# A mixture-of-experts and attention kernel: the first phase without filled expert queues, with on-chip counts, sixteen row buffers and splits placed behind other work

## The chip, the cores and the metric

The kernel runs on one core of one Trainium2 chip. A core has five engines with a queue each: TensorE (PE; its weight loads are listed as PEld), VectorE (DVE), ScalarE (ACT), GpSimd (POOL) and SyncE (SP, which here only issues DMA transfers). The metric is the device time in microseconds (us), the median of several executions. Before the change it is 1846.73 us (three runs, 1844.07 to 1847.13).

## The reference

The input `x` has 4096 tokens of 256 floats. Three steps are added to it one after the other: half a feed-forward layer, attention in groups of 64 tokens, half the same feed-forward layer again.

```python
x = x + 0.5 * ffn(layernorm(x))
x = x + attention(layernorm(x))     # groups of 64 tokens, 16 heads, causal
x = x + 0.5 * ffn(layernorm(x))

def ffn(x):                         # T = 4096 tokens, H = 256, E = 8 experts, 2 per token
    logits = rmsnorm(x) @ router_w.T
    p2, i2 = top_k(softmax(logits), 2);  rw = p2 / p2.sum()
    # each expert takes its first 640 tokens in order, the rest is dropped
    for e in experts:
        xg = x[dispatch[e]]                              # 640 x 256
        out = (silu(xg @ rg[e]) * (xg @ ru[e])) @ rd[e]  # 1024 hidden
        routed[dispatch[e]] += out * weight[e]
    shared = (silu(x @ sg) * (x @ su)) @ sd              # 2048 hidden, all tokens
    return shared + routed
```

## The kernel before

Each float32 operand of a matmul is split into a high and a low float16 plane, and three products (high-high, high-low, low-high, `TERMS`) stand for one. The split of a weight is one operation on ACT (high plane) and one on DVE (low plane): `split`, L102 and L103.

There are four phases, each a `with n.phase(...)` block. Phase a normalises all 32 tiles of 128 tokens, routes them, and runs the shared experts over the first four blocks of 512 tokens. Phase b runs the eight experts for the first layer. Phase c runs attention for 32 tiles, the routing of the second layer, and eleven blocks of shared experts. Phase d runs the experts of the second layer and the last shared block.

The **shared experts** of a block (`shared`) go in 16 chunks of 128 hidden units. A chunk is `gate_up` (twelve matmuls of 128x512 into two PSUM tiles `pgu`, L302; then silu on ACT, L313, into `sl`; product on DVE, L315; high plane `hh` on ACT, L317; low plane `hl` on DVE, L318) and `down` (twelve matmuls of 128x256 into `po`, L326). `down` of a chunk is deferred until `gate_up` of the next chunk has been issued.

The **front** of a tile (`tile1`, `front_steps`): load `y` (L629), statistics on DVE (L137 to L140), a power on POOL (L142), normalised `z` (L154), the two planes into a row buffer `X` (`two`: ACT L162, DVE L163), a transpose into `xb` (on PE for the first block, `turn`; by DMA for the others, L172), router matmuls and a copy of the logits on ACT (L207). After every fourth tile `route` picks the two best experts, counts positions with matmuls against a running count `run`, and computes the destination rows `di` (L268). `scatter` then writes four tag columns into `X` on POOL (L281: token number, two weights, first expert) and sends the 128 rows to the experts' queues `xg` in DRAM, twice, with an indirect DMA from POOL (L283). `X` has ten buffers in phase a, so the eleventh tile reuses the first one's once its scatters have landed.

The queues are **filled** beforehand (`fill`, L738 to L745): for each expert a zeroed tile with a token number beyond the end (so that an unused slot is dropped on the way back) is written to `xg`. The fill of the first layer stands in front of the blocks, that of the second layer beside block 2. The scatters of a layer come after its fills.

An **expert's load** (`expert_load`) reads a transposed copy of the queue (`xe`, L373) and the tag columns (`tag`, L375, two buffers), and makes the row indices `ids` on POOL (L380) and the weights `w` on DVE (L381, L383), each in two buffers. `experts` calls it for the next expert while one is computed; for the first expert it is called when all tiles are done.

Order of work: `Tiles.steps` advances the tiles that are alive; `drive` runs the yields of a shared block and lets the tiles take steps between them. The program text only gives a priority: a scheduler with a timeline of its own places each instruction on its engine's queue[...]. `issue_after` keeps an instruction behind another one in this placing. `load_shared` (L116) issues all loads and splits of the shared weights (8 steps of two chunks each, raw tiles in two buffers) before block 0 in the program's text.

Of the kernel before, what the change touches and what calls it, by code (L numbers as in the profile page):

```python
# [1 line left out]

# [18 lines left out]
P = 128  # L21
# [16 lines left out]
class Net:  # L38
    def __init__(self, ctx, tc):
        self.tc = tc  # L40
        self.nc = nc = tc.nc
        pool = lambda name, bufs, **k: ctx.enter_context(tc.tile_pool(name=name, bufs=bufs, **k))
        self.cst = pool("cst", 1)
        self.wsh = pool("wsh", 1)
        self.tok = pool("tok", YB)
        self.xb = pool("xb", NB)
        self.xe = pool("xe", 2)
        self.sm = pool("sm", 2)
        self.dr = pool("dr", 1, space=DRAM)
# [12 lines left out]
        for e in range(E):  # L62
            nc.gpsimd.memset(self.iota8[:, e:e + 1], float(e))
        self.mhalf = c.tile([P, 8], F32, name="mhalf")
        nc.gpsimd.memset(self.mhalf, -0.5)
        self.mone = c.tile([P, 4], F32, name="mone")
        nc.gpsimd.memset(self.mone, -1.0)
        self.e1 = c.tile([P, 4], F32, name="e1")
        nc.gpsimd.memset(self.e1, 2.718281828459045)
        tk = self.sm.tile([P, 32], I32, name="tk", bufs=1)  # L70
        nc.gpsimd.iota(tk, pattern=[[P, 32]], base=0, channel_multiplier=1)
        self.tokid = c.tile([P, 32], F32, name="tokid")
        nc.vector.tensor_copy(self.tokid, tk)
# [31 lines left out]

    def load_router(self, router_w):
        nc = self.nc
        r = self.raw.tile([E, H], F32, name="rtr", tag="raw2")
        nc.sync.dma_start(out=r, in_=router_w)
        self.rwt = self.cst.tile([P, 2, 2, E], F16, name="rwt")  # L110
        p = self.m1([P, 2, E], F32, "prt")
        for k in range(2):
            nc.tensor.transpose(p[:, k, :], r[:, k * P:(k + 1) * P], self.ident[:E, :E])
        self.split(self.rwt[:, 0], self.rwt[:, 1], p)

    def load_shared(self, sg, su, sd):  # L116

        nc = self.nc
        w = self.wsh
        self.sgu = w.tile([P, 16, 2, 2, 2, P], F16, name="sgu")  # L120
        self.sdw = w.tile([P, 2, 16, H], F16, name="sdw")
        for c in range(0, 16, 2):
            r = self.raw.tile([P, 2, 2, 2 * P], F32, name=f"rs{c}", tag="raw")
            for i, s in enumerate((sg, su)):
                nc.sync.dma_start(
                    out=r[:, i], in_=s[:, c * P:(c + 2) * P].rearrange("(k p) f -> p k f", p=P))
            for j in range(2):
                src = r[:, :, :, j * P:(j + 1) * P]
                self.split(self.sgu[:, c + j, 0], self.sgu[:, c + j, 1], src)
            r2 = self.raw.tile([P, 2, H], F32, name=f"rd{c}", tag="raw2")  # L130
            nc.sync.dma_start(out=r2, in_=sd[c * P:(c + 2) * P].rearrange("(k p) f -> p k f", p=P))
            self.split(self.sdw[:, 0, c:c + 2], self.sdw[:, 1, c:c + 2], r2)

    def stats(self, x, mv, rstd):
        nc = self.nc
# [5 lines left out]
            out=ve, in0=mv[:, 1:2], scalar1=LN_EPS, scalar2=1.0 / UP ** 2, op0=ALU.add, op1=ALU.mult)  # L141
        nc.gpsimd.tensor_tensor(out=rstd, in0=ve, in1=self.mhalf[:, :1], op=ALU.pow)  # L142

    def planes(self, x, xp, mv, rstd, pool=False):

        nc = self.nc
        z = self.tok.tile([P, H], F32, name="z", bufs=3)
        if pool:
            nm = self.sm.tile([P, 1], F32, name="nm")
            nc.vector.scalar_tensor_tensor(  # L150
# [2 lines left out]
        else:  # L153
            nc.vector.tensor_scalar(  # L154
                out=z, in0=x, scalar1=mv[:, 0:1], scalar2=rstd, op0=ALU.subtract, op1=ALU.mult)
        self.two(xp, z, pool)
        return z

    def two(self, xp, z, pool=False):
# [15 lines left out]
    def turn(self, z, xt):  # L175

        p = self.m1([P, 2, P], F32, "ptx")
        for k in range(2):
            self.nc.tensor.transpose(p[:, k, :], z[:, k * P:(k + 1) * P], self.ident)
        self.nc.scalar.copy(xt[:, 0:2], p)  # L180
        self.nc.vector.tensor_tensor(out=xt[:, 2:4], in0=p, in1=xt[:, 0:2], op=ALU.subtract)

    def front_new(self):
        fb = {"X": [None] * 4, "n": 0, "pe": False}
# [24 lines left out]
    def route(self, R, b, fb):  # L209
# [57 lines left out]
        di = sm.tile([P, 4, 2], I32, name="di")  # L267
        nc.vector.tensor_copy(di, df)  # L268
        yield
        for t in range(4):  # L270
            with self.tc.issue_after(self.anchor.ins) if self.anchor else nullcontext():
                self.scatter(R, b, fb, t, di, w1, dl, ef)
            yield

    def scatter(self, R, b, fb, t, di, w1, dl, ef):
        nc = self.nc
# [15 lines left out]
    def gate_up(self, wc, x, h, tanh=False):  # L292
# [4 lines left out]
        for i in range(2):  # L297
# [8 lines left out]
            if i == 0:  # L306
# [3 lines left out]
                    nc.vector.scalar_tensor_tensor(  # L310
                        out=s, in0=s, scalar=1.0, in1=p, op0=ALU.add, op1=ALU.mult)
                else:
                    nc.scalar.activation(s, p, AF.Silu, scale=1.0 / XP)  # L313
                yield
        nc.vector.scalar_tensor_tensor(  # L315
            out=s, in0=ps[1], scalar=1.0 / XP / (2.0 * XP if tanh else 1.0), in1=s, op0=ALU.mult, op1=ALU.mult)
        nc.scalar.copy(h[0], s)  # L317
        nc.vector.tensor_tensor(out=h[1], in0=s, in1=h[0], op=ALU.subtract)  # L318
        yield
# [49 lines left out]
    def expert_load(self, R, e, hold):  # L369
        nc = self.nc  # L370
        rows = R["xg"][e * CAP:(e + 1) * CAP]
        xt = hold["x"] = self.xe.tile([P, 4, CAP], F16, name="xe")
        nc.sync.dma_start_transpose(out=xt, in_=rows[:, 0:H].bitcast(F16))  # L373
        tag = self.sm.tile([P, 5, 4], F32, name="tag")
        nc.sync.dma_start(out=tag, in_=rows[:, H:XW].rearrange("(t p) f -> p t f", p=P))  # L375
        yield
        yield
        ids = hold["id"] = self.sm.tile([P, 5], I32, name="eid")
        w = hold["w"] = self.sm.tile([P, 5], F32, name="ew")
        nc.gpsimd.tensor_copy(ids, tag[:, :, 0])  # L380
        nc.vector.scalar_tensor_tensor(  # L381
            out=w, in0=tag[:, :, 3], scalar=float(e), in1=tag[:, :, 1], op0=ALU.is_equal, op1=ALU.mult)
        nc.vector.tensor_tensor(out=w, in0=w, in1=tag[:, :, 2], op=ALU.add)  # L383
# [85 lines left out]
    def attn_tile(self, R, j, x2, new_fb):  # L469
# [9 lines left out]
        self.stats(y, mv, rstd)  # L479
        yield  # L480
        xa = a.tile([P, 2 * H], F16, name="xa")
        self.planes(y, xa, mv, rstd, True)
        yield
        V2 = self.V2[j % 2]
        xt = self.flip(xa)
# [116 lines left out]
    def front_steps(self, y, t, new_fb, keep=None):  # L602
# [3 lines left out]
        X = self.xs.tile([P, XW], F32, name="X")  # L606
        xp = X[:, 0:H].bitcast(F16)
        fb["X"][t] = X
        z = self.planes(y, xp, fb["mv"][:, t, :], fb["rstd"][:, t:t + 1], keep is not None)
        xt = fb["xb"][:, :, t * P:(t + 1) * P]  # L610
        if fb["pe"]:
            self.turn(z, xt)
            fb["n"] += 1
            for _ in range((3 - t) * GAP_A + 1):
                yield
        if keep is not None:
            self.nc.sync.dma_start(out=keep, in_=y)
        yield
# [45 lines left out]
        self.slot += 1  # L664


def run_slots(tiles, until):
    while not until():
        for _ in tiles.steps():
# [23 lines left out]
def macaron(ctx, tc, x, w_qkv, ln_w, w_proj, router_w, rg, ru, rd, sg, su, sd, out):  # L693
# [7 lines left out]
    x2 = n.dr.tile([T, H], F32, name="x2")  # L701
    fbs = {}
    used = set()

    def new_fb(h, b):
        def get(t):
# [11 lines left out]
    def tile1(j):  # L718
        b, t = divmod(j, 4)
        y = n.load_tile(x, b, t)  # L720
        yield
        yield
        yield from n.front_steps(y, t, new_fb(1, b))
        yield from tail(R1, 1, b, t)

    def tile2(j):
        b, t = divmod(j, 4)
        yield from n.attn_tile(R1, j, x2 if b < NC else out, new_fb(2, b))
        yield from tail(R2, 2, b, t)

    def ready(h, b):
        return lambda: (h, b) in fbs and fbs[(h, b)]["n"] == 4
# [2 lines left out]
        yield from n.shared(b, fbs[key]["xb"], src, dst, **k)  # L735
        used.add(key)

    def fill(R):  # L738

        for e in range(E):  # L740
            z = n.raw.tile([P, 5, XW], F32, name="zero")
            nc.gpsimd.memset(z, 0.0)
            nc.vector.tensor_scalar_add(z[:, :, H], n.tokid[:, 0:5], float(T + e * CAP))
            nc.sync.dma_start(out=R["xg"][e * CAP:(e + 1) * CAP].rearrange("(t p) f -> p t f", p=P), in_=z)
            yield  # L745

    with n.phase("a", BT, 2, 10):
        n.ident = n.at.tile([P, P], F32, name="ident")
        make_identity(nc, n.ident)
        n.load_router(router_w)  # L750
        tiles = Tiles(tile1, 32, GAP_A)
        run_slots(tiles, ready(1, 0))
        n.load_shared(sg, su, sd)
        for _ in fill(R1):
            pass
        for b in range(NA):
            run_slots(tiles, ready(1, b))
            if b == 2:
                tiles.extra.append(fill(R2))
                for i in range(NA, NB):  # L760
                    nc.sync.dma_start(out=R1["acc"][i * BT:(i + 1) * BT], in_=x[i * BT:(i + 1) * BT])
            drive(all_shared((1, b), b, x, R1["acc"]), tiles, RATE_A)
        run_slots(tiles, tiles.done)
        cur = {}
        for _ in n.expert_load(R1, 0, cur):
            pass
    with n.phase("b", CAP, 3):
        n.experts(R1, rg, ru, rd, cur)
    with n.phase("c", BT, 2, 6, SLC):
        n.attn_init(w_qkv, ln_w, w_proj)  # L770
        tiles = Tiles(tile2, 32, GAP_C)
# [6 lines left out]
        cur = {}  # L778
        for _ in n.expert_load(R2, 0, cur):
            pass  # L780
    with n.phase("d", CAP, 3):
        n.experts(R2, rg, ru, rd, cur)
        for b in range(NC, NB):
            for _ in all_shared((2, b), b, out, out, late=10):
                pass
# [40 lines left out]
```

## Time and profile before

| What | Value |
|---|---|
| median of three runs | 1846.73 us |
| profiled execution | 1844.18 us, of which the span is 1842.5 us |
| phase a ends, phase b begins (PE) | 297.5 us |
| first matmul of shared experts | 14.10 us |
| granted PE clock | 0.999 of full speed |
| HBM | read 81.04 MB, written 52.85 MB |
| `xg<-zero` (fills) | 16 transfers of 650 KB |
| scatters L283 | 128, 1.03 us each on POOL |

The page gives per engine the busy time and its share of the span. A stage's row, as asked for by stretches of time, gives the same for a window. A wait is listed as "engine, line, waited for, us in total, times, longest". A row of the timeline is start, duration, engine, line, operation, output and inputs, count, and in brackets the idle time before it with what ended it.

### The profile page before, as it was taken

The numbers are of one execution on the slowest core, as the hardware profiler recorded it, in microseconds if no ns is written. First come the engines' busy times: TensorE is split into PE (matmuls) and PEld (weight loads), VectorE is DVE, ScalarE is ACT, GpSimd is POOL, SyncE is SP. The second block draws the span as 40 slices with busy tenths as digits, with TensorE's granted clock in tenths as the row PEclk, the third lists the DMA queues.
The fourth block names the chain that finished last, engine by engine and source line by source line (L and its number), as shares of the span: only waits on it lengthen the run. The fifth ranks groups of instructions, "written<-read, shape, count | busy, mean of one in ns | idle before, by whom it ended". The sixth has DMA issues, their size and how long they took to land.

```text
span 1842.5 us, 37619 instructions
## 1 busy us (share of the span) xinstructions
PE 1782.8 (97%) x13722; PEld 1197.0 (65%) x13722; DVE 1204.9 (65%) x2869; ACT 952.2 (52%) x2055; POOL 769.5 (42%) x1104
## 2 busy tenths in 40 slices
PE   6989999999999899999999999999999999999999
PEld 3545656777777556666666666666665677777765
DVE  7665545666666567787877878787755565666643
ACT  5333324555555365766666666666333455555542
POOL 7776540111221244567667676776530011112210
PEclk9999999999999999999999999999999999999999
DMA  9753022445554246767585776757213044455420
GB/s 291 224 142 94 12 63 69 107 107 114 128 115 101 58 80 110 118 114 158 104 148 117 140 137 119 152 98 125 48 30 87 27 111 111 108 112 127 104 47 12
DMA packets 447514, 196.61 MB, mean 107 GB/s; under 512 B 302369, under 2 KB 444381, under 8 KB 447264
## 3 DMA queue, kind: packets, MB, share of 16 engines
q1 hardware_dynamic: 429664, 173.03, 42.7%
q0 software_dynamic: 17664, 21.17, 6.7%
q8 instruction: 107, 1.75, 0.4%
q14 instruction: 79, 0.65, 0.1%
HBM read 81.04 MB, written 52.85 MB: 73 GB/s over the span
## 4 chain that ended last, share of the span: by engine, by line
PE 57%; POOL 12%; issue 11%; DVE 10%; DMA 5%; ACT 4%; SPq 1%; POOLq 0%; DVEq 0%; another core or an unknown queue 0%; ACTq 0%
PE pgu L302 36%; PE po L326 18%; POOL xg L283 3%; DVE sl L315 2%; DVE sl L310 1%; POOL X L281 1%; DVE hl L318 1%; POOL rstd L142 1%; POOL S L546 1%; DMA y<-in_L_attn_x_dram 1%; ACT hh L317 1%; PE pqk L599 1%; ACT sl L309 1%; POOL e L557 1%; DMA xg<-X,di 1%
## 5 line engine op out<-in xcount | busy, mean ns | idle before, releaser
L302 PE MATMUL pgu<-xb,sgu 128*128 128x512 f16 x3072 | 743.5, 380 | 20.3 <-DVE sl L310 8.0
L317 ACT CAST hh<-sl 128x512 f16<-128x512 f32 (+2 forms) x512 | 272.9, 533 | 485.4 <-DVE sl L315 471.4
L302 PE MATMUL pgu<-xe,wc 128*128 128x384 f16 (+1 forms) x3072 | 497.0, 299 | 0.8
L302 PEld LDWEIGHTS <-sgu 128*128 128x128 f16 x3072 | 294.0, 98 | 295.7 <-issue 29.6
L315 DVE SCALAR_TENSOR_TENSOR sl<-pgu,sl 128x512 f32<-128x512 f32 (+2 forms) x512 | 300.6, 587 | 215.5 <-PE pgu L302 180.1
L318 DVE TENSOR_TENSOR hl<-sl,hh 128x512 f16<-128x512 f32 (+2 forms) x512 | 311.0, 608 | 160.1 <-ACT hh L317 153.3
L326 PEld LDWEIGHTS <-hh 128*128 128x128 f16 x3328 | 319.8, 98 | 114.9 <-ACT hh L317 13.9
L302 PEld LDWEIGHTS <-wc 128*128 128x128 f16 x3072 | 300.5, 98 | 94.1 <-issue 1.9
L326 PE MATMUL po<-sdw,hh 128*128 128x256 f16 x2048 | 349.9, 273 | 10.1 <-ACT hh L317 6.8
L326 PE MATMUL po<-sdw,hl 128*128 128x256 f16 x1024 | 247.5, 273 | 11.7 <-DVE hl L318 10.4
L326 PE MATMUL po<-wd,hh 128*128 128x256 f16 x1280 | 223.6, 273 | 0.0
L326 PEld LDWEIGHTS <-hl 128*128 128x128 f16 x1664 | 162.8, 98 | 57.2 <-DVE hl L318 23.3
L422 POOL DMA_INDIRECT out_dram<-eo,eid x40 | 64.1, 1604 | 314.3 <-DVE hl L318 244.9
L313 ACT ACTIVATE sl<-pgu 128x384 f32<-128x384 f32 (+1 forms) x336 | 158.9, 473 | 56.7 <-PE pgu L302 27.6
L422 POOL DMA_INDIRECT acc<-eo,eid x40 | 64.8, 1621 | 266.2 <-DVE hl L318 227.4
L283 POOL DMA_INDIRECT xg<-X,di x128 | 131.3, 1026 | 66.2 <-issue 27.5
L326 PE MATMUL po<-wd,hl 128*128 128x256 f16 x640 | 152.5, 273 | 2.1 <-DVE hl L318 1.9
L310 DVE SCALAR_TENSOR_TENSOR sl<-sl,pgu 128x512 f32<-128x512 f32 x176 | 120.0, 682 | 45.4 <-ACT sl L309 43.2
L309 ACT ACTIVATE sl<-pgu 128x512 f32<-128x512 f32 x176 | 104.3, 593 | 42.3 <-PE pgu L302 36.3
L102 ACT ACTIVATE wc<-re 128x512 f16<-128x512 f32 x128 | 80.5, 629 | 78.0 <-PE pgu L302 51.2
L103 DVE SCALAR_TENSOR_TENSOR wc<-re,wc 128x512 f16<-128x512 f32 x128 | 88.3, 690 | 25.9 <-ACT wc L102 25.7
L546 POOL TENSOR_TENSOR S<-S,amx 128x1024 f32<-128x1024 f32 x32 | 62.1, 1939 | 79.1 <-DVE amx L545 72.1
(141 smaller groups left out, 1740.6 us busy)
## 6 DMA issues: line engine op xcount, KB each, us to landing
re<-in_L_ffn_rg_dram SPq DMA_DIRECT2D x128, 128.0 KB
re<-in_L_ffn_ru_dram SPq DMA_DIRECT2D x128, 128.0 KB
re<-in_L_ffn_rd_dram SPq DMA_DIRECT2D x128, 128.0 KB
xg<-zero SPq DMA_DIRECT2D x16, 650.0 KB
y<-acc SPq DMA_DIRECT2D x64, 128.0 KB
y<-in_L_attn_x_dram SPq DMA_DIRECT2D x32, 128.0 KB
acc<-xr SPq DMA_DIRECT2D x16, 256.0 KB
out_dram<-xr SPq DMA_DIRECT2D x16, 256.0 KB
```

The source lines that it names most:

```text
L103: nc.vector.scalar_tensor_tensor(out=lo, in0=src, scalar=WS, in1=hi, op0=ALU.mult, op1=ALU.subtract)
L283: i = nc.gpsimd.indirect_dma_start(out=R["xg"][:, :], out_offset=bass.IndirectOffsetOnAxis(ap=di[:, t, k:k + 1], axis=0), in_=X, in_offset ...
L302: nc.tensor.matmul(p, lhsT=wc[:, w, i, k, :], rhs=x[:, 2 * a + k, :], start=(j == 0), stop=(j == 5))
L309: nc.scalar.activation(s, p, AF.Tanh, scale=0.5 / XP)
L310: nc.vector.scalar_tensor_tensor(out=s, in0=s, scalar=1.0, in1=p, op0=ALU.add, op1=ALU.mult)
L313: nc.scalar.activation(s, p, AF.Silu, scale=1.0 / XP)
L315: nc.vector.scalar_tensor_tensor(out=s, in0=ps[1], scalar=1.0 / XP / (2.0 * XP if tanh else 1.0), in1=s, op0=ALU.mult, op1=ALU.mult)
L317: nc.scalar.copy(h[0], s)
L318: nc.vector.tensor_tensor(out=h[1], in0=s, in1=h[0], op=ALU.subtract)
L326: nc.tensor.matmul(o, lhsT=h[a][:, t * P:(t + 1) * P], rhs=wd[:, w], start=(c == 0 and j == 0 and t % 2 == 0), stop=(c == nch - 1 and j == 2),
L422: i = nc.gpsimd.indirect_dma_start(out=R["acc"][:, :], out_offset=bass.IndirectOffsetOnAxis(ap=ids[:, t:t + 1], axis=0), in_=eo, in_offset ...
L546: self.anchor = nc.gpsimd.tensor_tensor(out=S, in0=S, in1=mx.unsqueeze(2).to_broadcast([P, 16, 64]), op=ALU.subtract)
```

## The change

In the first phase:

- The fills are gone. Instead `limits` counts after the last block how many rows each expert has, makes a bit mask and an offset for each slot on the chip, and `expert_load` applies them to the token numbers that it reads: a slot that was not written gets a number beyond the end. This is done on DVE; `ids` and `w` get a buffer of their own for each expert and layer, and the tag is loaded ahead of the transposed rows.
- `X` has 16 buffers, `z` has five instead of three, the raw weight tiles have four instead of two.
- `load_shared` is a generator. Its first step is called ahead of the router's load and issues the first weights from ACT's queue; their splits follow when the first block's front is done. The others are taken one step in six yields of block 0 (`fed`), and their splits are placed behind the latest silu, product or copy (`behind`, `latest`). In the tiles that are transposed on PE, the planes in `X` come behind the transposed copies.
- The copies of `x` into `acc` for the later four blocks are written tile by tile from `y`, not by four copies inside DRAM.
- A first `Silu` on eight columns stands at the start.
- The first expert's load is called at the end of the last tile, in phases a and c.

```diff
+        warm = c.tile([P, 8], F32, name="warm")
+        nc.scalar.activation(warm, self.mhalf, AF.Silu)
...
         for c in range(0, 16, 2):
-            r = self.raw.tile([P, 2, 2, 2 * P], F32, name=f"rs{c}", tag="raw")
+            issue = nc.sync if c else nc.scalar
+            r = self.raw.tile([P, 2, 2, 2 * P], F32, name=f"rs{c}", tag="raw", bufs=4)
             for i, s in enumerate((sg, su)):
-                nc.sync.dma_start(
+                issue.dma_start(
                     out=r[:, i], in_=s[:, c * P:(c + 2) * P].rearrange("(k p) f -> p k f", p=P))
...
+            r2 = self.raw.tile([P, 2, H], F32, name=f"rd{c}", tag="raw2", bufs=4)
+            issue.dma_start(out=r2, in_=sd[c * P:(c + 2) * P].rearrange("(k p) f -> p k f", p=P))
+            if c == 0:
+                yield
+            with self.behind(True, *((1,) if c == 0 else (0, 1))):
+                for j in range(2):
+                    src = r[:, :, :, j * P:(j + 1) * P]
+                    self.split(self.sgu[:, c + j, 0], self.sgu[:, c + j, 1], src)
+                self.split(self.sdw[:, 0, c:c + 2], self.sdw[:, 1, c:c + 2], r2)
+            yield
...
+    @contextmanager
+    def behind(self, on=True, *engines):
+        with ExitStack() as st:
+            if on:
+                for k in engines:
+                    st.enter_context(self.tc.issue_after(self.latest[k]))
+            yield
...
+        if b == NB - 1:
+            self.limits(R)
+            yield
...
+    def limits(self, R):
+        nc = self.nc
+        p = self.m1([P, E], F32, "pn")
+        nc.tensor.matmul(p, lhsT=self.ones, rhs=R["run"], start=True, stop=True)
+        taken = self.sm.tile([P, E, 5], F32, name="taken", bufs=1)
+        nc.vector.tensor_tensor(
+            out=taken, in0=self.tokid[:, 0:5].unsqueeze(1).to_broadcast([P, E, 5]),
+            in1=p.unsqueeze(2).to_broadcast([P, E, 5]), op=ALU.is_lt)
+        R["bits"] = self.cst.tile([P, E, 5], I32, name=R["key"] + "b")
+        nc.vector.tensor_scalar_mul(R["bits"], taken, -1.0)
+        R["off"] = self.cst.tile([P, E, 5], F32, name=R["key"] + "o")
+        nc.vector.tensor_scalar(
+            out=R["off"], in0=taken, scalar1=-8192.0, scalar2=8192.0, op0=ALU.mult, op1=ALU.add)
...
     def expert_load(self, R, e, hold):
+        tag = self.sm.tile([P, 5, 4], F32, name="tag")
+        nc.sync.dma_start(out=tag, in_=rows[:, H:XW].rearrange("(t p) f -> p t f", p=P))
         xt = hold["x"] = self.xe.tile([P, 4, CAP], F16, name="xe")
         nc.sync.dma_start_transpose(out=xt, in_=rows[:, 0:H].bitcast(F16))
-        tag = self.sm.tile([P, 5, 4], F32, name="tag")
-        nc.sync.dma_start(out=tag, in_=rows[:, H:XW].rearrange("(t p) f -> p t f", p=P))
...
-        ids = hold["id"] = self.sm.tile([P, 5], I32, name="eid")
-        w = hold["w"] = self.sm.tile([P, 5], F32, name="ew")
-        nc.gpsimd.tensor_copy(ids, tag[:, :, 0])
+        ids = hold["id"] = self.cst.tile([P, 5], I32, name=f"eid{R['key']}{e}")
+        w = hold["w"] = self.cst.tile([P, 5], F32, name=f"ew{R['key']}{e}")
+        tk = self.sm.tile([P, 5], I32, name="tkb")
+        nc.vector.tensor_tensor(out=tk, in0=tag[:, :, 0].bitcast(I32), in1=R["bits"][:, e], op=ALU.bitwise_and)
+        nc.vector.tensor_tensor(out=ids, in0=tk.bitcast(F32), in1=R["off"][:, e], op=ALU.add)
...
             self.turn(z, xt)
             fb["n"] += 1
             for _ in range((3 - t) * GAP_A + 1):
                 yield
+        with self.behind(fb["pe"], 0, 1):
+            self.two(xp, z, keep is not None)
...
+def fed(main, weights):
+    for i, _ in enumerate(main):
+        if i % 6 == 0:
+            next(weights, None)
+        yield
...
+        if b >= NA:
+            nc.sync.dma_start(out=R1["acc"][j * P:(j + 1) * P], in_=y)
         yield from n.front_steps(y, t, new_fb(1, b))
         yield from tail(R1, 1, b, t)
+        if j == 31:
+            yield from n.expert_load(R1, 0, first[0])
...
-    with n.phase("a", BT, 2, 10):
+    with n.phase("a", BT, 2, 16):
         n.ident = n.at.tile([P, P], F32, name="ident")
         make_identity(nc, n.ident)
+        weights = n.load_shared(sg, su, sd)
+        next(weights)
         n.load_router(router_w)
         tiles = Tiles(tile1, 32, GAP_A)
         run_slots(tiles, ready(1, 0))
-        n.load_shared(sg, su, sd)
-        for _ in fill(R1):
-            pass
+        next(weights)
         for b in range(NA):
             run_slots(tiles, ready(1, b))
-            if b == 2:
-                tiles.extra.append(fill(R2))
-                for i in range(NA, NB):
-                    nc.sync.dma_start(out=R1["acc"][i * BT:(i + 1) * BT], in_=x[i * BT:(i + 1) * BT])
-            drive(all_shared((1, b), b, x, R1["acc"]), tiles, RATE_A)
+            main = all_shared((1, b), b, x, R1["acc"])
+            drive(fed(main, weights) if b == 0 else main, tiles, RATE_A)
```

More of the change, by code (lines that the diff above doesn't have):

```diff
@@ L1 @@
-from contextlib import ExitStack, nullcontext
+from contextlib import ExitStack, contextmanager, nullcontext
 import concourse.bass as bass
@@ L107, in load_router @@
         nc = self.nc
-        r = self.raw.tile([E, H], F32, name="rtr", tag="raw2")
+        r = self.raw.tile([E, H], F32, name="rtr", bufs=1)
         nc.sync.dma_start(out=r, in_=router_w)
@@ L122, in load_shared @@
         for c in range(0, 16, 2):
-            r = self.raw.tile([P, 2, 2, 2 * P], F32, name=f"rs{c}", tag="raw")
+            issue = nc.sync if c else nc.scalar
+            r = self.raw.tile([P, 2, 2, 2 * P], F32, name=f"rs{c}", tag="raw", bufs=4)
             for i, s in enumerate((sg, su)):
-                nc.sync.dma_start(
+                issue.dma_start(
                     out=r[:, i], in_=s[:, c * P:(c + 2) * P].rearrange("(k p) f -> p k f", p=P))
[L127 to L132, printed above, removed]
+            r2 = self.raw.tile([P, 2, H], F32, name=f"rd{c}", tag="raw2", bufs=4)
[8 more added lines that the diff above has]
+            yield
     def stats(self, x, mv, rstd):
@@ L142, in stats, with normed @@
         nc.gpsimd.tensor_tensor(out=rstd, in0=ve, in1=self.mhalf[:, :1], op=ALU.pow)
-    def planes(self, x, xp, mv, rstd, pool=False):
+    def normed(self, x, mv, rstd, pool=False):
         nc = self.nc
-        z = self.tok.tile([P, H], F32, name="z", bufs=3)
+        z = self.tok.tile([P, H], F32, name="z", bufs=5)
         if pool:
@@ L155, in planes @@
                 out=z, in0=x, scalar1=mv[:, 0:1], scalar2=rstd, op0=ALU.subtract, op1=ALU.mult)
-        self.two(xp, z, pool)
         return z
@@ L179, in turn @@
             self.nc.tensor.transpose(p[:, k, :], z[:, k * P:(k + 1) * P], self.ident)
-        self.nc.scalar.copy(xt[:, 0:2], p)
-        self.nc.vector.tensor_tensor(out=xt[:, 2:4], in0=p, in1=xt[:, 0:2], op=ALU.subtract)
+        i = self.nc.scalar.copy(xt[:, 0:2], p)
+        j = self.nc.vector.tensor_tensor(out=xt[:, 2:4], in0=p, in1=xt[:, 0:2], op=ALU.subtract)
+        self.latest = [i.ins, j.ins]
+    @contextmanager
[5 more added lines that the diff above has]
+            yield
     def front_new(self):
@@ L312, in gate_up @@
                 else:
-                    nc.scalar.activation(s, p, AF.Silu, scale=1.0 / XP)
+                    self.latest[0] = nc.scalar.activation(s, p, AF.Silu, scale=1.0 / XP).ins
                 yield
-        nc.vector.scalar_tensor_tensor(
-            out=s, in0=ps[1], scalar=1.0 / XP / (2.0 * XP if tanh else 1.0), in1=s, op0=ALU.mult, op1=ALU.mult)
+        self.latest[1] = nc.vector.scalar_tensor_tensor(
+            out=s, in0=ps[1], scalar=1.0 / XP / (2.0 * XP if tanh else 1.0), in1=s, op0=ALU.mult, op1=ALU.mult).ins
         nc.scalar.copy(h[0], s)
@@ L481, in attn_tile @@
         xa = a.tile([P, 2 * H], F16, name="xa")
-        self.planes(y, xa, mv, rstd, True)
+        self.two(xa, self.normed(y, mv, rstd, True), True)
         yield
@@ L608, in front_steps @@
         fb["X"][t] = X
-        z = self.planes(y, xp, fb["mv"][:, t, :], fb["rstd"][:, t:t + 1], keep is not None)
+        z = self.normed(y, fb["mv"][:, t, :], fb["rstd"][:, t:t + 1], keep is not None)
         xt = fb["xb"][:, :, t * P:(t + 1) * P]
@@ L664, in steps @@
         self.slot += 1
+def fed(main, weights):
+    for i, _ in enumerate(main):
+        if i % 6 == 0:
+            next(weights, None)
+        yield
 def run_slots(tiles, until):
@@ L703, in macaron @@
     used = set()
+    first = {}, {}
     def new_fb(h, b):
@@ L729, in tile2 @@
         yield from tail(R2, 2, b, t)
+        if j == 31:
+            yield from n.expert_load(R2, 0, first[1])
     def ready(h, b):
@@ L736, in all_shared @@
         used.add(key)
[L738 to L745, printed above, removed]
-    with n.phase("a", BT, 2, 10):
+    with n.phase("a", BT, 2, 16):
         n.ident = n.at.tile([P, P], F32, name="ident")
         make_identity(nc, n.ident)
+        weights = n.load_shared(sg, su, sd)
+        next(weights)
         n.load_router(router_w)
@@ L752, in macaron @@
         run_slots(tiles, ready(1, 0))
-        n.load_shared(sg, su, sd)
-        for _ in fill(R1):
-            pass
+        next(weights)
         for b in range(NA):
             run_slots(tiles, ready(1, b))
-            if b == 2:
-                tiles.extra.append(fill(R2))
-                for i in range(NA, NB):
-                    nc.sync.dma_start(out=R1["acc"][i * BT:(i + 1) * BT], in_=x[i * BT:(i + 1) * BT])
-            drive(all_shared((1, b), b, x, R1["acc"]), tiles, RATE_A)
+            main = all_shared((1, b), b, x, R1["acc"])
+            drive(fed(main, weights) if b == 0 else main, tiles, RATE_A)
         run_slots(tiles, tiles.done)
-        cur = {}
-        for _ in n.expert_load(R1, 0, cur):
-            pass
     with n.phase("b", CAP, 3):
-        n.experts(R1, rg, ru, rd, cur)
+        n.experts(R1, rg, ru, rd, first[0])
     with n.phase("c", BT, 2, 6, SLC):
@@ L777, in macaron @@
         run_slots(tiles, tiles.done)
-        cur = {}
-        for _ in n.expert_load(R2, 0, cur):
-            pass
     with n.phase("d", CAP, 3):
-        n.experts(R2, rg, ru, rd, cur)
+        n.experts(R2, rg, ru, rd, first[1])
         for b in range(NC, NB):
```

## The prediction

> **What bounds the kernel now.** I read the page's busy time first, then the busy time by stage, then single waits in the timeline, since a share over the whole span hides a stage.
>
> ```profile
> PE 1782.8 (97%) x13722; PEld 1197.0 (65%) x13722; DVE 1204.9 (65%) x2869; ACT 952.2 (52%) x2055; POOL 769.5 (42%) x1104
> ```
>
> TensorE (PE) is the bound of the whole, so only what takes idle time from PE counts. The change reaches the first phase, which ends near 298 us. The start of the VectorE (DVE) product L315 marks each of its 64 chunks: chunk 1 at 25.16, chunk 16 at 88.96, chunk 32 at 165.72, chunk 64 at 297.81. The same stretches by engine (us, then PE, PEld, DVE, ACT, POOL busy with counts, clock, DMA share, GB/s):
>
> ```profile
> 0.00:25.00 25.00, 11.68 (x58) 5.26 (x59) 18.11 (x64) 11.96 (x28) 14.47 (x48) 1.00 0.89 267
> 25.00:89.00 64.00, 58.65 (x399) 34.32 (x398) 48.20 (x166) 28.49 (x61) 49.64 (x85) 1.00 0.87 251
> 89.00:166.00 77.00, 68.00 (x449) 39.63 (x450) 45.21 (x151) 23.47 (x53) 56.05 (x123) 0.98 0.44 122
> 166.00:298.00 132.00, 128.18 (x855) 76.71 (x853) 62.08 (x162) 42.68 (x85) 52.31 (x109) 1.00 0.23 53
> ```
>
> An undisturbed chunk takes 3.90 us (first pgu pieces at 284.55, 288.44, 292.35). So 63 chunks cost 245.7 us of the 272.7 between first and last mark; router matmuls (28 tiles at 0.16 us) add some 5. About 22 us are stalls, and a further 25 pass before the first mark. The largest excess is in the second block of 16 chunks: 76.8 us where 62.4 would do. Its cause stands in ScalarE's (ACT) chain of waits and in PE's timeline:
>
> ```profile
> ACT X L162 <- DMA xg<-X,di: 42.6, 18, 6.2
> 95.50 0.61 PE L326 MATMUL po<-sdw,hh 128*128 128x256 f16 x4 [1.65 <-ACT X L162]
> 120.51 0.59 PE L302 MATMUL pgu<-xb,sgu 128*128 128x512 f16 x2 [2.24 <-DVE sl L315]
> ```
>
> A row buffer X can't be rewritten until its scatter has landed (18 waits, 42.6 us), ACT stands on it, and hh behind it is late for PE. The first scatter starts only at 61.70, because all eight fills of xg must land first.
>
> [...] at 94.5 us ACT waits 6.17 us for one X and hh follows it. [...] this trace has 1.28 us twice, the second at 21.12 ahead of the first Silu. [...]
>
> **The change part by part.** I use the instruction order of the changed program as built, with durations from this trace.
>
> *Start and block 0.* No zero memsets (1.19 us each) stand ahead of ident; the first Silu table load (1.28) moves to idle time; the first weights leave from ACT. But chunk 1's mark stands on DVE behind the statistics of tile 8, whose y load has 4.5 MB ahead of it (seven y, three weight sets of 768 KB on SP, one on ACT, 512 KB of xr). At some 275 GB/s (the 267 above, 320 at its peak) that is 16.4 us, plus about 2.5 of issue and landing: mark at 19, against 25.2. From there DVE decides. A 512-wide operation costs it 0.60 us start to start, a 256-wide 0.34, a small one some 0.17. By that count it has 74.4 us to do up to mark 16, against 69.1 before (where the trace has 66.3 busy): the 24 splits lie as before inside the block, and front work of later tiles joins them. Fifteen sections between marks come to 3.6, 4.4, 4.4, 4.0, 4.0, 4.2, 6.2, 2.8, 7.2, 2.0, 4.7, 6.1, 2.5, 4.2, 2.3. PE can't go below 3.9 per chunk; taking the larger of both gives 68.9. The same rule gives some 65 for before, measured 63.8, so I take 67.5. Mark 16 falls at 86.5: **-2.5 us**. Bounds: with the light sections fully used by a DVE that is behind, 60 us, -10; with hl late for PE after each heavy section, 72, +2. SP's queue loses eight fills and four 512 KB copies and gains sixteen 128 KB stores, none ahead of a load in time of need.
>
> *Block 1.* Sixteen buffers put the first reuse at tile 17, whose X stands in section 11, about 64 us. Tile 1's scatter follows the destination indices in section 9 (about 55; POOL has nothing left of the fill before it), costs 1.3 each for two and lands 2.3 later: 60, in time by 4 us. The later rows stand 2 to 5 us behind their scatters, at one chunk per 3.9. So the block falls to 62.4 + 1.8 of router work + 1.8 for evictions and one heavy section = 66: **-10.8**, or -7 if half the margins are missed.
>
> *Blocks 2 and 3.* 132.1 us before, with 124.8 of chunks; PE idle there is under 4 us, most of it at the hand-over. No change apart from that.
>
> *The hand-over to the experts.* This part isn't in the few words of the change. ids and w now have a buffer per expert, so nothing holds back the tag loads of later experts: the built order puts all eight between chunks 56 and 60, and DVE, not POOL, reads them. Only two tag buffers exist, so tags 5 and 6 wait for DVE to read 3 and 4, and 7 and 8 for 5 and 6, while DVE stands in its queue ahead of hl of chunks 59 and 60. SP's queue and DVE of before at that place:
>
> ```profile
> 274.11 0.58 SPq L375 DMA_DIRECT2D tag<-xg  x1
> 279.48 0.95 SPq L375 DMA_DIRECT2D tag<-xg  x2
> 278.73 0.17 DVE L381 SCALAR_TENSOR_TENSOR ew<-tag 128x5 f32<-128x5 f32 x1 [3.06 <-DMA tag<-xg]
> 279.76 0.28 PE L326 MATMUL po<-sdw,hl 128*128 128x256 f16 x1 [2.15 <-DVE hl L318]
> ```
>
> A tag takes from its issue to its use 2.7, 4.6, 2.5 and 2.6 us in four places of this trace. With r for that time, hl of chunk 60 ends near 279.5 + 3r + 2.3; PE took it at 287.57, so PE waits 3r - 5.8: 2.1 at 2.65, 8.1 at 4.65. I take r = 3: **+3.5**. What's late next is only gate_up of chunk 62, and with it the phase's end. On the other side, tag now leaves ahead of the 2.8 us transposing load, so the 3.06 and 2.15 above go: **-2**. At the second hand-over, near 1385, the order is the same with hl of the last two chunks behind the tags; 1.73 of idle before it hangs on a weight load and stays: **+2.5** (1 to 6).
>
> *Costed at nothing:* the counts (one matmul, three operations of 40 elements; hidden by PE work in chunks 54 to 57, 0.8 us if not); two more DVE operations per expert (0.2 us each); in the expert phases and the attention phase the built order is the same but for the tags, now absent from seven later places where nothing waited.
>
> Sum: -2.5 - 10.8 + 3.5 - 2 + 2.5 = -9.3. The profiled execution, 1844.18 us (1842.5 span plus 1.7), becomes 1834.9; the median of the runs stands 2.5 above it, so I expect 1837.4.
>
> **The rivals.**
> *Small gain or none (within 0.2%, 3.7 us).* The rows' wait is replaced, not removed: splits ahead of the index arithmetic delay tile 1's scatter by more than its 4 us, ACT stands again, and block 1 gives only 7 while the lumps of block 0 give +2: about -1, 1846. For it: DVE has more work in block 0 than before. Against: the fill kept the first scatter until 61.70, and that wait is gone for certain.
> *Large gain.* DVE's backlog is worked off in its light sections (block 0: -10) and the tags stay in the slack that PE leaves hl (po of a chunk follows gate_up of the next, 3.9 us later, and sl, hh, hl take 2.0: 1.9 us): -10 - 10.8 - 2 + 3, near -19, 1827. For it: in 38.9 to 60.4 before, DVE did five sections of 20.6 us in 21.5. Against: heavy sections end with hl, which PE needs.
> *Slower.* The tag rounds. At both hand-overs the price is about 3r - 6 each, 6r - 12 together; what the first phase gains is 15.3, so it decides from r = 4.5. At r = 5.2 it costs 19, +4: 1851. For it: the 4.6 was seen with other loads about, and four tags now leave back to back. Against: three of four were 2.7 or less, and these loads are 10 KB.
> *That the fill was hidden anyway* and nothing moves is excluded by the 42.6 us and PE's stalls behind them, save as part of the first rival.
>
> **How the numbers follow.** The forecast (-4 to -14) has 0.58, small gain or none 0.17, large gain 0.14, slower 0.11. The forecast's own range is 1833 to 1843. From the unknown costs (block 0 -10 to +2, block 1 -12 to -7, tags +3 to +14) the range for 8 in 10 is 1827 to 1848. A difference of 0.2% is about what a measurement of this kernel can tell from no change. Faster 0.72, same 0.17, slower 0.11.
>
> **What would show it.** Mark 1 of the product after L315's counterpart near 19; mark 16 near 86 with DVE over 90% busy; mark 32 near 152 with no wait of ACT for the scatters above 1 us; two waits of DVE on tags of 2 to 3 us near 270, each followed by PE waiting on hl. Wrong would be: marks 1 to 16 in under 62 us (DVE's lumps don't reach PE), waits of ACT for scatters remaining in block 1, or PE idle above 8 us at either hand-over.

## The result and the profile after

The changed kernel takes 1833.97 us (median of four runs, 1832.14 to 1834.99) against 1846.25 for the kernel before beside it: ratio 0.9931, interval 0.9916 to 0.9947. The forecast was 1837.4, range 1827 to 1848. The profiled execution took 1834.82 us, its span 1833.1 (before: 1844.18 and 1842.5).

"Mark k" is, as in the prediction, the start of the k-th product on DVE, now L349; "block 0" is marks 1 to 16, "block 1" marks 16 to 32. The busy line of the page after:

```profile
PE 1779.5 (97%) x13724; PEld 1197.0 (65%) x13724; DVE 1199.9 (65%) x2891; ACT 952.9 (52%) x2055; POOL 751.3 (41%) x1072
```

PE does the same work. Of the 9.4 us by which the span is shorter, 6.1 are PE's idle time; its busy time falls by 3.3 with nearly the same matmuls, and the runs don't show why. The stretches between the marks of after (us, then PE, PEld, DVE, ACT, POOL busy with counts, clock, DMA share, GB/s):

```profile
0.00:16.50 16.50, 8.86 (x50) 4.32 (x51) 10.03 (x45) 6.32 (x16) 8.63 (x42) 1.00 0.92 315
16.50:85.50 69.00, 61.02 (x422) 36.28 (x421) 57.08 (x202) 36.31 (x83) 50.84 (x96) 1.00 0.57 156
85.50:157.00 71.50, 65.45 (x435) 38.44 (x434) 39.09 (x126) 23.02 (x50) 44.95 (x107) 0.98 0.34 88
157.00:291.00 134.00, 128.76 (x859) 77.16 (x857) 62.21 (x184) 41.21 (x79) 51.74 (x103) 1.00 0.21 47
```

| us | mark 1 | mark 16 | mark 32 | mark 64 | block 0 | block 1 |
|---|---|---|---|---|---|---|
| before | 25.16 | 88.96 | 165.72 | 297.81 | 63.8 | 76.8 |
| after | 16.59 | 85.69 | 156.94 | 290.65 | 69.1 | 71.3 |
| predicted | 19 | 86.5 | 152 | – | 67.5 | 66 |

The gain is made by mark 32 (8.8 us), and by the marks nearly all of it is the earlier start (8.6 us). From mark 1 to mark 32 it is 140.6 us before and 140.4 after (138.9 in a second profile of the changed kernel, e5): block 1 gives half of what was forecast, and block 0, which is longer than before, takes most of that back. The chain of waits, first 300 us of after (engine, line, waited for, us in total, times, longest):

```profile
ACT X L168 <- DMA xg<-X,di: 23.3, 10, 3.8
...
DVE z L161 <- POOL rstd L149: 10.7, 6, 4.0
...
DVE tkb L416 <- DMA tag<-xg: 4.4, 6, 1.4
```

The rows' wait (42.6 us before) has nearly halved, not gone. DVE's wait for the power `rstd` from POOL has grown (2.4 us in two places before). Its waits for tags come in six places where they came in two, but they aren't longer in sum (5.2 us before). Single rows of after's timeline (start, duration, engine, line, operation; in brackets the idle time before it and its releaser):

```profile
55.98 1.37 POOL L317 DMA_INDIRECT xg<-X,di  x1 [0.19 <-ACT sl L347]
66.41 0.97 POOL L317 DMA_INDIRECT xg<-X,di  x1 [0.30 <-issue]
68.29 0.57 POOL L149 TENSOR_TENSOR rstd<-ve,mhalf 128x1 f32<-128x1 f32 x1
68.89 0.41 DVE L161 TENSOR_SCALAR z<-y,mv,rstd 128x256 f32<-128x256 f32 x1 [3.99 <-POOL rstd L149]
72.57 0.28 PE L360 MATMUL po<-sdw,hl 128*128 128x256 f16 x1 [1.70 <-DVE hl L352]
105.96 0.40 ACT L168 CAST X<-z 128x256 f16<-128x256 f32 x1 [3.13 <-DMA xg<-X,di]
112.46 0.43 DVE L169 TENSOR_TENSOR X<-z,X 128x256 f16<-128x256 f32 x1 [3.08 <-DMA xg<-X,di]
113.55 0.59 PE L336 MATMUL pgu<-xb,sgu 128*128 128x512 f16 x2 [2.39 <-DVE sl L349]
```

The first scatter starts 5.7 us earlier than before (61.70). But a block's eight scatters follow each other on POOL, until 67.4, and the `rstd` of a later tile stands behind them, at 68.29, though its input `ve` was made at 58.55; z, hl and PE follow. At 112.46 DVE has waited 3.08 us for a row, the product sl stands behind it, and at 113.55 PE has lost 2.39 us. Something follows that the prediction didn't count (stretches of after, columns as above):

```profile
112.00:115.00 3.00, 1.39 (x6) 0.61 (x6) 1.86 (x4) 1.88 (x5) 1.11 (x5) 0.85 0.35 88
115.00:118.00 3.00, 3.00 (x15) 1.76 (x14) 1.80 (x6) 0.62 (x1) 0.00 (x0) 0.58 0.22 44
118.00:121.00 3.00, 3.00 (x27) 2.04 (x26) 1.39 (x8) 1.38 (x3) 0.27 (x2) 1.00 0.00 0
```

After the stall the granted clock is at about half (0.50 from 115 to 117 us) for some 3.4 us: 3 x 0.15 + 3 x 0.42 = 1.7 us of full clock are lost on top of the 2.39. At the first hand-over, the tags of the last four experts leave in two pairs, at 273.34 and 274.01 and at 276.50 and 276.96 (the first row below puts the four together). Three of their reads wait, for 1.45, 1.06 and 0.64 us:

```profile
273.34 4.09 SPq L407 DMA_DIRECT2D tag<-xg  x4
276.03 0.17 DVE L416 TENSOR_TENSOR tkb<-tag,scatter0b 128x5 int32<-128x5 int32 x1 [1.45 <-DMA tag<-xg]
280.40 0.28 PE L360 MATMUL po<-sdw,hl 128*128 128x256 f16 x1 [1.03 <-DVE hl L352]
```

### The profile page after: what moved, and what is told of

Its sections match the earlier page's. It is cut to its first block, busy times and chain, and to the rows that moved or that the text cites. A ratio compares the mean times of both kernels' runs of the same rounds, so it can differ in the third digit from the quotient of the medians.

```text
span 1833.1 us, 37526 instructions
## 1 busy us (share of the span) xinstructions
PE 1779.5 (97%) x13724; PEld 1197.0 (65%) x13724; DVE 1199.9 (65%) x2891; ACT 952.9 (52%) x2055; POOL 751.3 (41%) x1072
## 4 chain that ended last, share of the span: by engine, by line
PE 36%; issue 32%; POOL 12%; DVE 10%; DMA 5%; ACT 4%; SPq 0%; POOLq 0%; another core or an unknown queue 0%; DVEq 0%; ACTq 0%
PE pgu L336 22%; PE po L360 11%; POOL xg L317 3%; DVE sl L349 2%; DMA acc<-eo,eidscatter 2%; DVE sl L344 1%; DVE hl L352 1%; POOL X L315 1%; POOL rstd L149 1%; POOL acc L459 1%; ACT hh L351 1%; PE pqk L636 1%; POOL S L583 1%; DVE st L144 1%; POOL e L594 1%
## 5 line engine op out<-in xcount | busy, mean ns | idle before, releaser
L349 DVE SCALAR_TENSOR_TENSOR sl<-pgu,sl 128x512 f32<-128x512 f32 (+2 forms) x512 | 300.2, 587 | 227.3 <-PE pgu L336 193.4
L360 PE MATMUL po<-sdw,hl 128*128 128x256 f16 x1024 | 247.1, 273 | 14.3 <-DVE hl L352 13.4
L459 POOL DMA_INDIRECT out_dram<-eo,eidscatter x40 | 65.1, 1627 | 342.1 <-DVE eo L458 332.3
L459 POOL DMA_INDIRECT acc<-eo,eidscatter x40 | 65.7, 1643 | 296.5 <-DVE eo L458 286.8
```

What stands on the lines that cost most here:

```text
L349: self.latest[1] = nc.vector.scalar_tensor_tensor(out=s, in0=ps[1], scalar=1.0 / XP / (2.0 * XP if tanh else 1.0), in1=s, op0=ALU.mult, op ...
L360: nc.tensor.matmul(o, lhsT=h[a][:, t * P:(t + 1) * P], rhs=wd[:, w], start=(c == 0 and j == 0 and t % 2 == 0), stop=(c == nch - 1 and j == 2),
L459: i = nc.gpsimd.indirect_dma_start(out=R["acc"][:, :], out_offset=bass.IndirectOffsetOnAxis(ap=ids[:, t:t + 1], axis=0), in_=eo, in_offset ...
```

## The experiments

Theory A is the prediction's: sixteen row buffers free block 1, and the tag rounds cost. Rivals B to E are named in the expectations, and e1 to e12 are the runs in the order in which they were made. All ratios are against runs of the kernel before taken beside the experiment; 0.001 is 1.84 us. Marks and waits come from one profiled execution of each kernel, which lies up to 2.6 us from the median of its runs (e9).

### Row buffers: ten, and twenty-four

```diff
-    with n.phase("a", BT, 2, 16):
+    with n.phase("a", BT, 2, 10):      # e2; 24 in e3 and e4
```

e4 also has, after each tile's scatters of the first layer, `for _ in range(8): yield`.

> The changed kernel with ten row buffers in place of sixteen. Theory A (sixteen buffers are what took ScalarE's waits for scatters out of block 1): the gain of that block, 5.5 us, goes and a little of block 0 with it: 1840 to 1845, ScalarE's waits for scatters up from 23 us to 40 or more. Rival B (without the fill the first scatter starts 5.7 us earlier, and that alone freed the rows): 1834 to 1836, waits near 25 us.

Measured: 1829.19 us, 0.9926 (0.9913 to 0.9939). Nothing is lost by going back to ten buffers. Its waits in the first 300 us, and its block 1:

```profile
ACT X L168 <- DMA xg<-X,di: 36.0, 19, 4.3
```

```profile
86.50:152.00 65.50, 61.90 (x429) 37.15 (x428) 39.50 (x132) 22.41 (x49) 42.91 (x98) 1.00 0.32 90
```

ACT's waits for scatters rise from 23.3 to 36.0 us, nearly as far as theory A expected, and yet block 1 takes 65.5 us with the clock at 1.00, less than with sixteen. Theory A falls: the sum of these waits was no measure of what PE loses. Rival B has the time (it expected 0.994 or so), though not the waits.

> The changed kernel with 24 row buffers, so that no tile of block 1 meets a scatter that hasn't landed. Theory A (the rows are what is left of block 1's stalls): the 23 us of ScalarE's waits for scatters fall under 5, the sixteen chunks of block 1 take 66 to 67 us instead of 71.25, median 1829 to 1830. Rival C (GpSimd's run of eight scatters keeps the power of the statistics waiting, and z, the planes and hl behind it): waits of VectorE for that power stay near 7 us in block 0 and 3.5 in block 1, block 1 takes 69.5 or more, median 1832.5 to 1834.5.

Measured: 1827.41 us, 0.9915 (0.9902 to 0.9928). No wait for scatters is left on ACT, and block 1 takes 67.6 us. Theory A has the rows and nearly the time, rival C the power; each is half right. Two rows of its timeline, and two stretches:

```profile
69.98 0.44 DVE L161 TENSOR_SCALAR z<-y,mv,rstd 128x256 f32<-128x256 f32 x1 [5.11 <-POOL rstd L149]
...
73.71 0.28 PE L360 MATMUL po<-sdw,hl 128*128 128x256 f16 x1 [4.29 <-DVE hl L352]
```

```profile
74.00:77.00 3.00, 3.00 (x13) 1.39 (x12) 3.00 (x15) 1.51 (x5) 2.78 (x13) 0.62 0.40 96
77.00:80.00 3.00, 3.00 (x15) 1.48 (x14) 3.00 (x12) 1.83 (x4) 2.51 (x6) 0.81 0.59 164
```

With the rows free, the power behind POOL's scatters is the wait (14.1 us in six places), PE stalls 4.29 us, and the clock takes another (0.38 + 0.19) x 3 = 1.7.

> 24 row buffers and eight more pauses between the scatters of one tile and of the next in the first layer: the built order has the first run of eight scatters on GpSimd broken into four, two and two, with other tiles' work between; the next runs stay at eight. Theory A (rows only): as with 24 buffers alone, within 1 us. Rival C (the runs of scatters hold the power): the wait of VectorE for the power near 69 us, 4.0 us before, goes, and the median is 1 to 3 us under the one with 24 buffers alone.

Measured: 1826.93 us, 0.9915 (0.9902 to 0.9929), the same as e3. It doesn't tell the theories apart. The run of eight scatters was broken into four, two and two, but only a short operation of the routing stood in each break. From 56.87 to 69.6 no power came between the scatters, and DVE waited 5.35 us for one at 70.88. Taking the power off POOL wasn't tried.

### The fill alone, and the fill put back

With this input the router sends 948 to 1132 rows to each queue of 640 slots in the first layer and 919 to 1112 in the second (counted with the reference's router), so no slot shows the fill's value. e7 and e8 leave the default for unwritten slots out.

```diff
-        for _ in fill(R1):
-            pass
...
-                tiles.extra.append(fill(R2))
```

> The kernel before without the two fills; ten row buffers and all else as before. Theory D (the fill alone held the first scatters and with them the rows of block 1): mark 1 near 21, first scatter near 56, the chunks of block 1 66 to 70 us instead of 76.8, median 8 to 11 us under before. Rival (the buffers decide, theory A of the forecast): mark 1 gains 3 to 4 and block 1 stays near 74, median 3 to 5 us under before.

> The kernel before without the two fills and with sixteen row buffers. Theory D: no faster than with ten, or up to 5 us slower. Theory A of the forecast: 5 to 8 us faster than with ten, block 1 near 66 us.

Measured: e7 1830.49 us, 0.9931 (0.9919 to 0.9944); e8, with sixteen buffers, 1829.45 us, 0.9929 (0.9913 to 0.9946). Beside them the changed kernel:

> The changed kernel as it is, beside the others of this call and the kernel before, so that effects of 1 to 5 us are read on one chip. All theories: 0.993 of the kernel before. If two tag buffers cost what theory A says, it is 2 to 4 us above the same kernel with eight; if not, within 1 us of it.

Measured: 1831.34 us, 0.9938 (0.9925 to 0.9950). **Without the two fills, the kernel before gains as much as with the whole change.** e7's gain is above its expectation (12.7 us by the ratio). Its first scatter starts at 53.58. e8 is faster than e7 by 0.4 us of the ratio, which the intervals can't tell from nothing, as theory D had it. Blocks 0 and 1 of e7:

```profile
21.50:88.50 67.00, 61.22 (x409) 36.23 (x408) 50.98 (x170) 30.45 (x67) 47.14 (x95) 0.97 0.59 155
88.50:155.50 67.00, 64.27 (x444) 38.28 (x442) 40.15 (x133) 22.15 (x49) 42.70 (x99) 1.00 0.29 79
```

Block 1 falls from 76.8 to 66.9 us with ten buffers. Mark 32 is at 155.27, against 156.94 and 155.76 in the changed kernel's two profiles.

How does the fill cost? By the order scatter after fill, or by itself? In e9 it is all there, but writes to buffers that nothing reads:

```diff
-            nc.sync.dma_start(out=R["xg"][e * CAP:(e + 1) * CAP]..., in_=z)
+            nc.sync.dma_start(out=other[R["key"]][e * CAP:(e + 1) * CAP]..., in_=z)
```

> The kernel before with both fills written to other DRAM buffers that nothing reads: the same memsets and the same 10.4 MB of transfers, but no scatter has to follow a fill. Theory D1 (the order scatter after fill is what cost: first scatter at 61.70): first scatter near 54 to 56, block 1 near 67 us, mark 1 still near 25, median 7 to 9 us under before. Rival D2 (the traffic and the instructions of the fill cost, by late y loads and late statistics): median 0 to 3 us under before, block 1 above 73.

Measured: 1840.33 us, 0.9982 (0.9975 to 0.9990). The median is nearly what D2 expected (3.3 us by the ratio), the profile what D1 did: first scatter at 48.21, block 1 as short as in e7. Its blocks 0 and 1:

```profile
24.50:94.50 70.00, 62.53 (x421) 36.47 (x421) 54.08 (x177) 29.73 (x65) 58.04 (x103) 1.00 0.88 251
94.50:162.00 67.50, 61.34 (x422) 36.78 (x421) 40.70 (x140) 22.22 (x49) 45.94 (x100) 1.00 0.40 116
```

So the order lengthens block 1. But without it block 0 takes 69.8 us where the kernel before takes 63.8: of the 9.1 us gained in block 1, 6.0 come back in block 0. By the ratios, three quarters of the 12.7 us come only when the fill's own work goes too: mark 1 is at 24.72 in e9 and 21.67 in e7, block 0 takes 69.8 and 66.7 us, and in block 0 the DMA engines are at 0.88 and 0.59. The profile of e9 is one of its fastest executions, 2.6 us under its median, so its marks flatter it. Before, DVE also stood for POOL's memsets (group of the kernel before, first 95 us: busy us, mean ns, idle before it and what ended that):

```profile
L743 DVE TENSOR_SCALAR zero<-tokid 128x5 f32<-128x5 f32 x14 | 2.6, 182 | 5.0 <-POOL zero L742 4.8
```

These are 7.6 us of DVE's queue, with sl and hl behind them. Whether this or the transfers count for more isn't settled; no run separates them.

e11 puts both fills back into the changed kernel (`fill` and the lines above, as additions).

> The changed kernel with both fills put back where the kernel before has them, all else as changed. Theory D (the fill is the whole effect): the first scatter goes back to 62 or later and the median to 0.997 to 1.003 of the kernel before. Rival (the other parts are worth half): 0.994 to 0.996.

Measured: 1836.35 us, 0.9957 (0.9944 to 0.9970), in the rival's range, and the first scatter comes at 51.60, not at 62. The fill isn't the whole of it in this direction: all the other parts are worth 7.9 us when it is there. They are worth nothing when it is gone (1831.34 with them, 1830.49 without). 12.7 and 7.9 make 20.6 apart and 11.4 to 12.7 together. The marks (in brackets the difference to before) tell where each gains:

| us | mark 1 | marks 1 to 32 | mark 32 |
|---|---|---|---|
| before | 25.16 | 140.6 | 165.72 |
| no fill (e7) | 21.67 (-3.5) | 133.6 (-7.0) | 155.27 (-10.5) |
| fill elsewhere (e9) | 24.72 (-0.4) | 137.5 (-3.1) | 162.20 (-3.5) |
| other parts, with fill (e11) | 18.13 (-7.0) | 141.6 (+1.0) | 159.72 (-6.0) |
| the change | 16.59 (-8.6) | 140.4 (-0.2) | 156.94 (-8.8) |
| the change (e5) | 16.83 (-8.3) | 138.9 (-1.6) | 155.76 (-10.0) |
| the change, ten rows (e2) | 17.48 (-7.7) | 134.6 (-6.0) | 152.03 (-13.7) |
| the change, 24 rows (e3) | 16.87 (-8.3) | 135.0 (-5.6) | 151.87 (-13.9) |

The missing fill mainly shortens marks 1 to 32, the other parts the start. With both, the earlier start stays and the gain from mark 1 to mark 32 is nearly lost. With ten or 24 buffers more of it is kept: 134.4 to 137.4 us in the five profiles (e2, e3, e4, e6, e12), against 138.9 to 140.4 in the four with sixteen (after, e1, e5, e10). Why sixteen are placed worst isn't shown. With the fill back, block 1 takes 74.8 us although the first scatter is early and ACT waits only 7.5 us for rows. There the power stands behind the second run of eight scatters, the last of which ends at 92.2:

```profile
92.22 1.13 POOL L149 TENSOR_TENSOR rstd<-ve,mhalf 128x1 f32<-128x1 f32 x2
92.86 1.77 DVE L161 TENSOR_SCALAR z<-y,mv,rstd 128x256 f32<-128x256 f32 x1 [5.52 <-issue]
95.66 4.44 PE L336 MATMUL pgu<-xb,sgu 128*128 128x512 f16 x12 [3.27 <-DVE ve L147]
```

### The tag buffers and the splits

```diff
-        tag = self.sm.tile([P, 5, 4], F32, name="tag")
+        tag = self.sm.tile([P, 5, 4], F32, name="tag", bufs=8)
```

> The changed kernel with eight tag buffers in place of two, nothing else. Theory A (the tag rounds cost TensorE time at both hand-overs, some 2 and 3.5 us): all eight tags are in flight together, VectorE waits once for them instead of two or three times, and the median falls from 1834.0 to 1828 to 1831. Rival (hl has slack behind the tags, so the waits of VectorE there are hidden): 1833 to 1835.

Measured: 1828.45 us, 0.9923 (0.9910 to 0.9935). Against the changed kernel's 0.9931 and 0.9938 this is 1.5 to 2.8 us, between theory A and the rival; the intervals overlap. Two more pairs give 1.5 us (e6 against e2) and 1.3 us (e12 against e3). At the first hand-over little of it is seen: from mark 60 to mark 64 it takes 12.70 us, the changed kernel 13.91 and 13.53, but from mark 54 to mark 64 43.3 us, the changed kernel 44.2 and 43.3. The wait has moved ahead of mark 60. At the second it is clear: the last sixteen chunks of phase c take, from product to product, 60.1 to 60.6 us in the three profiles with eight tag buffers, 61.4 to 61.8 in the seven of the changed kernel and its variants with two, and 59.9 before.

> The changed kernel with ten row buffers in place of sixteen and eight tag buffers in place of two. Theory D (sixteen buffers as placed cost some 5 us by mark 32, through a stall of TensorE and a lower granted clock after it; and two tag buffers cost 2 to 4): 5 to 8 us under the changed kernel of the same call, block 1 near 65.5 us and no clock under 1.00 up to 157 us. Rival (the difference of the marks seen with ten buffers is chance of one execution): within 1.5 us of the changed kernel with eight tag buffers, 1 to 3 under the changed kernel.

Measured: 1827.06 us, 0.9918 (0.9901 to 0.9935), 4.3 us under the changed kernel beside it (e5) by the medians, block 1 65.6 us. Block 0 is 71.8 long, so mark 32 (155.35) is hardly earlier than in the changed kernel; the 152.03 of e2 didn't come again. That sixteen buffers cost 5 us, as theory D has it, isn't shown. In three pairs (e2 and the changed kernel, e6 and e1, e7 and e8) ten and sixteen differ by 0.4 to 2.2 us, with overlapping intervals, so no gain of sixteen over ten is seen.

e10 takes all weights' steps ahead of block 0 (`for _ in weights: pass`, and `drive(main, ...)` without `fed`).

> The changed kernel with all loads and splits of the shared weights ahead of block 0 in the program's text, not one step in six yields; sixteen row buffers, two tag buffers as changed. Theory E (the splits inside block 0 and the early start cancel: start -5 against the kernel before without fills, block 0 +2.4): mark 1 later by 2 to 5, block 0 shorter by as much, median within 1.5 us of the changed kernel (0.993 to 0.994 of before). Rival (placing them behind other work in block 0 is worth something of its own): 3 us or more above the changed kernel.

Measured: 1835.40 us, 0.9950 (0.9937 to 0.9962), 2.2 to 3.5 us above the changed kernel, with overlapping intervals; mark 1 at 19.97, block 0 71.7 us. Block 0 did not get shorter, so theory E's cancelling is not what happens. Placing the splits later may be worth a little of its own, but with these intervals that isn't shown.

### Both remedies together

24 row buffers and eight tag buffers, both edits as above.

> The changed kernel with 24 row buffers and eight tag buffers. If the two gains add (0.9915 with 24 row buffers, 0.9923 with eight tag buffers, 0.9931 to 0.9938 without either): 0.990 to 0.9915 of the kernel before, some 1825 to 1828 us. If they overlap, as the fill and the rest of the change do: 0.9915 to 0.992, no better than 24 row buffers alone. VectorE waits for tags once or twice at each hand-over, no wait for scatters in block 1.

Measured: 1829.64 us against 1845.25, 0.9908 (0.9894 to 0.9921): 17 us under the kernel before by the ratio, in the range for gains that add, though the interval reaches into the other range as well. It is the best ratio of all; the intervals of e1 to e4 and of e6 overlap it. The power's wait is still there (5.09 us at 71.23).

## Why the prediction was right in its sum, and where not

The profiled sum was -9.3 and came to -9.4 us; by the medians the gain is 12.3. That the sums agree so closely is luck: up to mark 32 the forecast was -13.3 and the profile has -8.8, and all that follows was to cost 4.0 and gave 0.6. Terms were wrong and made up for each other.

- *Start, -6.2 at mark 1:* measured -8.6. The mechanism holds (mark 1 stands right behind statistics whose y load ended DVE's wait at 16.24), the rate was mis-sized: 315 GB/s instead of 275, so the 4.5 MB take 14.3 us and not 16.4. That the set on ACT's queue counts among what is ahead of the y load was the author's estimate; no run separates it.
- *Block 0, 67.5 us from DVE's count:* measured 69.1. DVE was busy 57.08 of 69.0 us, 83% and not over 90%: waits for rows and for the power, which the count did not have, stand among its work. The count was too high as well: it had 74.4 us of work up to mark 16, where DVE was busy for 67.1 (before, 69.1 stood for 66.3 busy). So DVE's work isn't what decided the block's length. Both terms together: -3.3 for -2.5.
- *Block 1, -10.8 from sixteen buffers:* measured -5.5, and -6.9 in the second profile. The step that failed is "sixteen buffers put the first reuse at tile 17 ... The later rows stand 2 to 5 us behind their scatters". Rows still waited (3.13 us at 105.96), and the prediction's own sign of error, waits of ACT for scatters left in block 1, appeared. The size was reached with ten buffers (76.8 to 65.5 in e2, to 66.9 in e7), and missed with sixteen and the fill (74.8 in e11). Sixteen buffers were neither needed nor enough; the fill had to go. The reading of 42.6 us of ACT's waits as the thing to remove was the error behind it.
- *What was left out:* POOL's scatters as a run that other tiles' powers stand behind (3.99 us at 68.89), the clock after a stall of PE (about half for 3.4 us after the 2.39 at 113.55), and the fill's own work in block 0, which was priced at the start only. By e9's ratio that work is the larger part.
- *First hand-over, +3.5 - 2, second +2.5:* the first cost about the net of 1.5 (marks 54 to 64: 42.1 us before, 44.2 and 43.3 after), but eight tag buffers bring little back there, so that two of them were the cause isn't shown. At the second the mechanism holds: two tag buffers cost 1.5 to 1.8 us, eight 0.2 to 0.7. In all, eight give back 1.3 to 2.8 us, where 6 was the price of two. The rounds that waited took 2.0 to 2.7 us from issue to use and not 3, and the waits at the first hand-over were 1.45, 1.06 and 0.64, not two of 2 to 3. The forecast's own formula gives 3.2 at r = 3, not 3.5.
- *From mark 64 to the end* the change was to cost 2.5; the profiles have 1544.7 before and 1542.5 after. e7, which doesn't touch the tags, has 1542.6, so this difference isn't the change's; where before's execution lost it stays open.
- *The rivals:* "hidden anyway" was rightly excluded, and more strongly than argued. "Large gain" (whose terms make -19.8) needed a block 0 shorter by 10 us; it grew by 5.3. "Slower" needed 4.5 us per tag; no such round was seen. "Small gain" named splits ahead of the index arithmetic; the scatter came at 55.98, as forecast, so that mechanism didn't act.

## What to carry to other kernels

Before the terms of a change with many parts are added up, test the parts alone: here one part alone gave everything, the rest alone gave nearly two thirds of it, and together they gave no more, though the marks show them gaining at different places. Where one stall goes, another can take its room: here rows (ACT's 42.6 us before), then the power behind the scatters (DVE's 14.1 us in e3). The sum of a queue's waits says little; follow each to the first engine that bounds the stage. Initialising a buffer in DRAM cost twice here, through the order that it forces (9.1 us of block 1 in e9) and through the engines and transfers that it occupies (9.4 us by the ratios of e7 and e9).

## What the runs showed of the hardware

A long stall of TensorE mostly cost more than its length. Between 14 and 160 us of the fourteen profiles (before, after and the twelve runs) PE waited 18 times for over 2.0 us at a stretch. In 14 of these the granted clock fell by about 0.5 for 3.4 us (6.8 us with the wait of 4.56 us in e4). Half of 3.4 us, up to 1.7 us, is then lost on top of the wait. In e4, e7 and e8 it fell before the wait was over, and that part cost nothing: in e4 2.7 of the 6.8 us, which leaves 2.1 us lost. After 2.04, 2.06, 2.13 and 2.67 us it didn't fall. After the waits of 1.9 to 2.0 us it never did, and nowhere in that stretch did it fall without such a wait. From 160 us on, before and after have one more wait over 2.0 us, 2.15 (before, at 279.76), and it didn't fall there. So the length of a wait alone doesn't decide: a single wait of 2.07 us was followed by the fall (e12, at 95.35), one of 2.67 us wasn't (e6, at 80.91). What does decide isn't shown.

More buffers didn't simply make the kernel faster: ten, sixteen and 24 rows gave 0.9926, 0.9931 to 0.9938 and 0.9915, and in the same order 0.9918, 0.9923 and 0.9908 with eight tag buffers; most of the intervals overlap. With each, the placing of the whole first phase moves, and what is late next differs: rows above all with ten (36.0 us of ACT's waits in e2), rows and the power with sixteen (23.3 of ACT's and 10.7 of DVE's), the power without rows with 24 (14.1 of DVE's in e3).
